# Mixing's x loaded behind the store that frees its place, and more passes ahead of two waits, in a four-layer graph kernel

## The chip, the cores and the metric

The kernel runs on one core of a Trainium2 chip. Its time is the device time of that core in microseconds: 1966.11 us (median of three runs, 1965.88 to 1972.42). The profile is one execution with a span of 1961.8 us.

## The reference, cut to what matters

x is [8 batches, 2048 nodes, 64 features] and adj is a [2048, 2048] matrix of zeros and ones. Four graph layers follow one another, each as x = layernorm(x + layer(x)). The change lies in layer 0, with layer 1 beside it:

```python
# layer 0, its end
deg = max(adj.sum(-1), 1)
industry = einsum('nm,bmf->bnf', adj / deg, x @ W_ind)
g = einsum('bne,benf->bnf', coefs1, elu(all_he))        # from the hyperedges
pair = stack([industry, g])
coefs2 = softmax(tanh(pair @ fcW + fcb) @ av)           # over the two
out = coefs2[0] * industry + coefs2[1] * g
x = layernorm(x + out)
# layer 1
A = adj + I;  dinv = rsqrt(A.sum(1))
x = layernorm(x + (dinv * A * dinv) @ x @ W.T)
```

Layer 2 is a Chebyshev graph convolution with an adaptive adjacency, layer 3 runs three message-passing steps.

## The kernel before, in words

The adjacency stays on chip as 16 row tiles. Batches go in pairs p (four pairs, two batches of 64 features on 128 partitions), nodes in four chunks c of 512. Each x value is split into two parts for the matmuls (v0h/v0l to v3h/v3l, one pair of tiles for each chunk), so a product of a pair with the adjacency is 2 groups g of 64 matmuls in layer 0 (tiles ug) and as many again in each pair of layer 1 (tiles u). Each such matmul is called a **pass** here: `products` (L323) and `layer1` (L988) are generators that give one pass at a time, and `fill(n)` (L401) runs the next n passes between other work. TensorE's order is therefore written out by hand.

Two helpers place the other engines' work. `after(n, f, ...)` runs f when n further passes have been given (L298), and `pin` keeps an instruction in program order on its engine. DMA issues on SP, and instructions that are not pinned, are placed by the framework's planner, by its own estimate of when they are ready; the finished list of each engine is then run in order. A tile name with `bufs=2` has two places; a third tile of that name waits until the first is no longer used.

Stages that matter here:

- **Hyperedges** (about 100 to 230 us). For each node tile, g is made by TensorE (pz), VectorE (L774 to L783), ScalarE and GpSimd, and scattered to `gs_hbm` by an indirect DMA (L786). Passes of the products run between. Inside the products, `inverses` (L340) turns the degrees: TensorE transposes them (pdc), VectorE adds one (L347), GpSimd makes the power -1/2 (dinv, L348), VectorE takes the maximum with one and the reciprocal (L349, L350), and after 8 passes TensorE transposes them again (pinv), from where they go to `inv_hbm`.
- **Mixing** (about 234 to 505 us), 16 steps i, each one pair and chunk. `mix_load` fetches products and inverse degrees; `mix_ind` makes industry on TensorE (pi) and VectorE (L866); `mix_g` loads g (gn) and x (r), transposes g (pg) and copies it (gt, L881); `mix_scores` makes four matmuls pf in two halves, with tanh on ScalarE (L895), GpSimd's ind - gt (L902) and VectorE's differences (L900); `mix_weigh` makes pd and the weight (L912, L914); `mix_end` transposes back (pt), adds to r (add_up, L933), and normalizes r (L834 to L846, with GpSimd's power ln_r at L843) and stores it as x1 (L925). r also needs r += gn on GpSimd (L883), which `mix_g` asks for 8 passes after itself.
- **Layer 1** starts at about 314 us between mixing's steps. `l1_parts` loads x1 (y, L945), scales it on GpSimd (L948) and splits it on ScalarE (L166) and VectorE (L167). After 64 passes ScalarE copies the sums (ut, L1011) and `l1_end` multiplies them by W (po) and adds x1 (L967, L968), with another layernorm.

The loop (L1029) runs scores(i), end(i-1), load(i+2), ind(i+1), g(i+1), weigh(i), with 8 or 9 passes behind each part. The end of a step takes 18 passes from mix_end to the store.

Of the kernel before, what the change touches and what calls it, by code (L numbers as in the profile page):

```python
# [30 lines left out]
F32 = mybir.dt.float32  # L31
# [6 lines left out]
ALU = mybir.AluOpType  # L38
# [18 lines left out]
def tile_gnn_fast(  # L57
# [23 lines left out]
    nc = tc.nc  # L81
# [3 lines left out]
    P = 128  # L85
# [3 lines left out]
    NCH = N // C  # L89
    JT = C // P  # L90
# [12 lines left out]
    def evacuate(dst, src):  # L103

        turn[0] ^= 1
        if turn[0]:
            nc.scalar.copy(dst, src)
        else:
            nc.vector.tensor_copy(dst, src)
# [60 lines left out]
    def mm(*args, **kw):  # L170
        tc.keep_in_program_order(nc.tensor.matmul(*args, **kw))  # L171
# [40 lines left out]
    def adj_c(t, c):  # L212

        return adj[t][c // 2][:, cols(c % 2)]
# [69 lines left out]
    def load_x(dst, p, c, eng=nc.sync):  # L284

        load = eng.dma_start(dst, x_n[p, c])
        if eng is nc.gpsimd:
            tc.keep_in_program_order(load)
# [9 lines left out]
    def after(n, f, *more):  # L298

        soon.append([n, lambda: (f(), after(*more) if more else None)])  # L300
# [22 lines left out]
    def products():  # L323

        deg1 = hy.tile([P, NT], F32, name="deg1")

        def degrees(g):
            du = pph.tile([P, 2, C], F32, tag="ph", name=f"du{g}", bufs=2)
            for t in range(NT):
                for i in range(2):  # L330
                    mm(
                        du[:, i, :], lhsT=ones_r, rhs=adj_c(t, 2 * g + i), start=t == 0, stop=t == NT - 1
                    )
                    yield
            for i in range(2):
                c = 2 * g + i
                r = slice(c * P // NCH, (c + 1) * P // NCH)
                evacuate(deg4[r, :], du[r, i, :])

        def inverses():  # L340

            pdc = places["small"]([P, JT, P], "pdc")
            for j in range(JT):
                transpose(pdc[:, j, :], deg4[:, cols(j, P)])
            pdc = pdc.rearrange("p j (c r) -> p c j r", c=NCH)[:, :, :, 0]
            d1 = deg1.rearrange("p (c j) -> p c j", c=NCH)
            nc.vector.tensor_scalar(d1, pdc, 1.0, None, op0=ALU.add)  # L347
            nc.gpsimd.tensor_tensor(dinv, deg1, neg_half[:, :NT], ALU.pow)  # L348
            nc.vector.tensor_scalar(d1, pdc, 1.0, None, op0=ALU.max)  # L349
            nc.vector.reciprocal(deg1, deg1)  # L350
            for _ in range(8):
                yield
            for c in range(NCH):
                pt = places["small"]([P, C], "pinv")
                for j in range(JT):
                    k = c * JT + j
                    transpose(pt[:, cols(j, P)], deg1[:, k:k + 1].to_broadcast([P, P]))
                row = va.tile([P, C], F32, tag="ut", name="inv", bufs=2)
                nc.scalar.copy(row, pt)
                nc.sync.dma_start(inv_hbm[:, cols(c)], row)  # L360
                for _ in range(4):
                    yield

        for p in range(NP):
            for g in range(2):
                own = (2 * g, 2 * g + 1)
                ug = pph.tile([P, 2, C], F32, tag="ph", name="ug", bufs=2)
                u = {c: ug[:, c % 2, :] for c in own}
                turning = inverses() if p == 0 and g == 1 else iter(())
                for t in range(NT):  # L370
                    for i in range(2):
                        for c in own:
                            mm(
                                u[c], lhsT=part[t // JT][i][:, t % JT, :], rhs=adj_c(t, c),
                                start=t == 0 and i == 0, stop=t == NT - 1 and i == 1,
                            )
                            tick()
                            if t > 1:
                                next(turning, None)
                            yield  # L380
                    if p == NP - 1 and g == 1 and t % JT == JT - 1:
                        first_parts(t // JT, free)
                    if p + 1 < NP and t % JT == JT - 1:
                        c = t // JT
                        if g == 1:
                            parts(p + 1, c)
                        if g == 1 and c < 2 or g == 0 and c >= 2:
                            fetch(p + 1, (c + 2) % NCH)
                if p == NP - 1:

                    for t in range(g * NT // 2, (g + 1) * NT // 2):
                        onto_diagonal(t, nc.gpsimd, ALU.add)
                for c in own:
                    ut = va.tile([P, C], F32, tag="ut", name="ut", bufs=2)
                    nc.scalar.copy(ut, u[c])
                    nc.sync.dma_start(u0_hbm[p][:, cols(c)], ut)
                if p == 0 and g == 0:
                    yield from degrees(0)
                    yield from degrees(1)

    def fill(n):  # L401
        for _ in range(n):
            if next(filler, None) == "wait":
                tick()
# [11 lines left out]
    with tc.tile_pool(name="pa_ps", bufs=1, space=PSUM) as pps:  # L416
# [75 lines left out]
        gts = so.tile([P, BINS], F32, name="gts")  # L492
# [32 lines left out]
        for t in range(NT // 2):  # L525
            for k in range(2):
                r = slice(k * E, (k + 1) * E)
# [271 lines left out]
    mp = mix_scope.enter_context(tc.tile_pool(name="mix", bufs=1, side="right"))  # L799
# [12 lines left out]
    def wide(c):  # L812
        return slice(c * JT, (c + 1) * JT)

    uts, invs, gts, inds, tts, rs = {}, {}, {}, {}, {}, {}
    xn, done, stored, due = [], [0] * NP, set(), set()


    pin = tc.keep_in_program_order
# [30 lines left out]
    steps = NP * NCH  # L850
# [17 lines left out]
    def mix_g(i):  # L868

        p, c = divmod(i, NCH)  # L870
        gn = mp.tile([P, JT, P], F32, tag="gn", name="gn", bufs=2)
        nc.sync.dma_start(
            gn, gs_hbm.rearrange("(p t) f -> p t f", t=NT)[:, wide(c), p * P:(p + 1) * P]
        )
        rs[i] = mp.tile([P, JT, P], F32, tag="r", name="r", bufs=2)
        load_x(rs[i], p, c)
        pg = lps.tile([P, C], F32, tag="mm", name="pg", bufs=4)
        for j in range(JT):
            transpose(pg[:, cols(j, P)], gn[:, j, :])
        gts[i] = mp.tile([P, C], F32, tag="gt", name="gt", bufs=2)  # L880
        pin(nc.scalar.activation(gts[i], pg, AF.Identity, bias=-1.0))  # L881
        r = rs[i]
        after(8, lambda: pin(nc.gpsimd.tensor_tensor(r, r, gn, ALU.add)))  # L883

    def mix_scores(i):

        t1 = []
        for src in (inds[i], gts[i]):
            for b in range(2):

                s = slice(b * F, (b + 1) * F)
                pf = lps.tile([P, C], F32, tag="mm", name="pf", bufs=4)
                mm(pf, lhsT=fc2[s, :], rhs=src[s, :], start=True, stop=True)
                t1.append(mp.tile([P, C], F32, tag="t1", name="t1", bufs=4))
                pin(nc.scalar.activation(t1[-1], pf, AF.Tanh, bias=fcb_col))  # L895
        tts[i] = t1[0:2]

        def differences():
            for b in range(2):
                pin(nc.vector.tensor_tensor(t1[b], t1[b], t1[2 + b], ALU.subtract))  # L900

        pin(nc.gpsimd.tensor_tensor(inds[i], inds[i], gts[i], ALU.subtract))  # L902
        after(5, differences)

    def mix_weigh(i):

# [10 lines left out]
    def mix_end(i):  # L917
        p, c = divmod(i, NCH)
        r = rs.pop(i)
        pt = lps.tile([P, C], F32, tag="mm", name="pt", bufs=4)  # L920
        for j in range(JT):
            transpose(pt[:, cols(j, P)], inds[i][:, cols(j, P)])

        def end():
            nc.sync.dma_start(x1_hbm[p][:, wide(c), :], r)  # L925
            stored.add((p, c))
            if p == 0:
                first_parts(c, mixed)
            elif (p, c) in due:
                l1_parts(p, c)  # L930

        def add_up():
            pin(nc.vector.scalar_tensor_tensor(  # L933
                r, pt.rearrange("p (t f) -> p t f", f=P), 0.5, r, op0=ALU.mult, op1=ALU.add
            ))

        after(3, add_up, 0, *normalized(mp, r, r, False, end))
# [85 lines left out]
    mix_load(1)  # L1023
    fill(24)
    mix_ind(0)
    fill(12)
    mix_g(0)
    fill(4)
    for i in range(steps + 1):  # L1029
        k = 9 if i > NCH else 8  # L1030
# [299 lines left out]
    for p in range(NP):  # L1330
        for c in range(NCH):
            r = staged("r").rearrange("p t (b f) -> p t b f", f=F)
# [923 lines left out]
```

## Time and profile before

| what | value |
|---|---|
| time, median of 3 | 1966.11 us |
| span of the profile | 1961.8 us |
| TensorE busy | 1867.9 us (95%) |
| VectorE / GpSimd / ScalarE busy | 1004.3 / 529.5 / 392.7 us |
| mean granted TensorE clock | 0.984 |
| r += gn (L883) | 16 times, 1284 ns (median) |
| load of x (L286 into r) and store of x1 (L925) | 16 times each, 256 KB |

A row of a timeline names start, duration, engine, line, operation, the tile written and the tiles read; in brackets stands how long the engine had been idle and what ended that. A row of waits gives total microseconds, times, and the longest. A window row gives, after its length, the busy time of TensorE, of its weight loads, of VectorE, ScalarE and GpSimd, then the granted TensorE clock, the DMA share and GB/s. Where TensorE is at 10.00 in a window of 10 us, nothing else matters there; the interest is in the windows where it isn't.

### The profile page before, as it was taken

The numbers are of one execution on the slowest core, as the hardware profiler recorded it, in microseconds if no ns is written. First come the engines' busy times: TensorE is split into PE (matmuls) and PEld (weight loads), VectorE is DVE, ScalarE is ACT, GpSimd is POOL, SyncE is SP. The second block draws the span as 40 slices with busy tenths as digits, with TensorE's granted clock in tenths as the row PEclk, the third lists the DMA queues.
The fourth block names the chain that finished last, engine by engine and source line by source line (L and its number), as shares of the span: only waits on it lengthen the run. The fifth ranks groups of instructions, "written<-read, shape, count | busy, mean of one in ns | idle before, by whom it ended". The sixth has DMA issues, their size and how long they took to land.

```text
span 1961.8 us, 19565 instructions
## 1 busy us (share of the span) xinstructions
PE 1867.9 (95%) x7100; PEld 1211.1 (62%) x7100; DVE 1004.3 (51%) x1741; ACT 392.7 (20%) x771; POOL 529.5 (27%) x480
## 2 busy tenths in 40 slices
PE   6888899888899999999999999999999999999997
PEld 4666565555754444855665575566547787877875
DVE  7789555565532211356556736754785343343332
ACT  1455343333222121100000000000002121222211
POOL 3678644454454434311001101100001020100201
PEclk9999899999999999999999999999999999999999
DMA  9923333432500000311101111111111122121211
GB/s 322 308 87 107 121 129 126 127 118 80 175 6 27 25 3 22 119 38 60 48 33 43 57 52 33 46 57 35 43 33 35 43 55 54 44 54 49 54 27 24
DMA packets 94185, 143.10 MB, mean 73 GB/s; under 512 B 29232, under 2 KB 40112, under 8 KB 93696
## 3 DMA queue, kind: packets, MB, share of 16 engines
q1 hardware_dynamic: 83920, 105.39, 17.7%
q0 software_dynamic: 7760, 27.66, 4.2%
q10 hardware_dynamic: 2400, 8.72, 1.2%
q8 instruction: 58, 0.95, 0.2%
q14 instruction: 47, 0.39, 0.1%
HBM read 98.67 MB, written 43.06 MB: 72 GB/s over the span
## 4 chain that ended last, share of the span: by engine, by line
PE 76%; DMA 4%; POOL 3%; DVE 3%; issue 2%; ACT 1%; SPq 0%; POOLq 0%; ACTq 0%; DVEq 0%
PE u L171 34%; PE py L171 22%; PE ua L171 11%; PE pr L171 2%; PE ug L171 2%; POOL ln_r L843 1%; DMA x_hbm<-r 1%; PE po L171 1%; DMA r<-in_x_n 1%; PE pf L171 1%; PE pt L174 1%; PE s L171 1%; DVE r L846 0%; DMA gs_hbm<-acc,order 0%; POOL r L968 0%
## 5 line engine op out<-in xcount | busy, mean ns | idle before, releaser
L171 PE MATMUL py<-wp,xg 128*128 128x512 f32 x1024 | 475.2, 592 | 0.7 <-DMA xg<-u_hbm 0.7
L171 PEld LDWEIGHTS py<-wp,xg 128*128 128x128 f32 x1024 | 193.3, 189 | 161.4 <-issue 138.8
L1343 DVE TENSOR_TENSOR fcav<-py,emb_n 128x512 f32<-128x512 f32 x256 | 176.9, 691 | 135.0 <-PE py L171 129.1
L171 PE MATMUL ua<-pt,xn 128*128 128x512 f32 x512 | 230.2, 592 | 1.5 <-DVE pt L1124 1.5
L1344 DVE TENSOR_REDUCE r<-fcav 128x32 f32<-128x512 f32 x256 | 175.5, 686 | 8.2
L171 PEld LDWEIGHTS ua<-pt,xn 128*128 128x128 f32 x512 | 96.9, 190 | 111.2 <-issue 104.2
L154 POOL TENSOR_TENSOR ln_r<-ln_e,neg_half 128x8 f32<-128x8 f32 x32 | 53.5, 1671 | 399.4 <-DVE ln_e L152 370.0
L171 PE MATMUL u<-adj,v0h 128*128 128x512 f32 x384 | 147.7, 452 | 1.3 <-ACT h L1499 1.3
L171 PE MATMUL u<-adj,v2l 128*128 128x512 f32 x384 | 141.0, 432 | 1.3 <-DVE v2l L167 1.3
L171 PE MATMUL u<-adj,v2h 128*128 128x512 f32 x384 | 141.3, 434 | 0.0
L171 PE MATMUL u<-adj,v1h 128*128 128x512 f32 x384 | 140.8, 434 | 0.0
L171 PE MATMUL u<-adj,v0l 128*128 128x512 f32 x384 | 139.8, 431 | 0.0
L171 PE MATMUL u<-adj,v3l 128*128 128x512 f32 x384 | 138.9, 426 | 0.0
L171 PE MATMUL u<-adj,v1l 128*128 128x512 f32 x384 | 138.4, 427 | 0.0
L171 PE MATMUL u<-adj,v3h 128*128 128x512 f32 x384 | 138.4, 427 | 0.0
L1124 DVE TENSOR_SCALAR pt<-pt 128x512 f32<-128x512 f32 x64 | 30.3, 473 | 150.5 <-ACT pt L1123 150.3
L1130 POOL TENSOR_TENSOR acc<-acc,pt 128x512 f32<-128x512 f32 x60 | 76.5, 1275 | 107.0 <-DVE pt L1124 106.4
L1425 DVE SCALAR_TENSOR_TENSOR ar<-fcav,ar 128x512 f32<-128x512 f32 x64 | 46.8, 731 | 108.7 <-ACT ar L1424 108.7
L171 PEld LDWEIGHTS u<-adj,v0h 128*128 128x128 f32 x384 | 71.0, 189 | 36.7 <-issue 24.1
L171 PEld LDWEIGHTS u<-adj,v2l 128*128 128x128 f32 x384 | 72.8, 191 | 31.9 <-issue 15.9
L171 PEld LDWEIGHTS u<-adj,v1l 128*128 128x128 f32 x384 | 72.9, 190 | 29.3 <-issue 14.4
L171 PEld LDWEIGHTS u<-adj,v3l 128*128 128x128 f32 x384 | 72.1, 188 | 29.4 <-issue 14.9
(360 smaller groups left out, 2717.2 us busy)
## 6 DMA issues: line engine op xcount, KB each, us to landing
adj<-in_adj_t POOLq DMA_DIRECT2D x32, 512.0 KB, 8.0
fcav<-in_adj_t SPq DMA_DIRECT2D x64, 256.0 KB, 2.9
u_hbm<-ut SPq DMA_DIRECT2D x48, 256.0 KB, 2.8
xg<-u_hbm SPq DMA_DIRECT2D x96, 128.0 KB, 2.9
x_hbm<-r SPq DMA_DIRECT2D x28, 256.0 KB, 2.2
hs_hbm<-st ACTq DMA_DIRECT2D x8, 584.0 KB, 5.4
xt<-in_x_t SPq DMA_DIRECT2D x16, 256.0 KB, 6.1
ut<-u_hbm SPq DMA_DIRECT2D x16, 256.0 KB, 3.4
```

Of the source, the lines that this page charges most:

```text
L154: nc.gpsimd.tensor_tensor(rstd, vare, neg_half[:, :groups], ALU.pow)
L171: tc.keep_in_program_order(nc.tensor.matmul(*args, **kw))
L174: tc.keep_in_program_order(nc.tensor.transpose(dst, src, ident))
L843: pin(nc.gpsimd.tensor_tensor(rstd, vare, neg_half[:, :groups], ALU.pow))
L1124: nc.vector.tensor_scalar(pt, pt, 1.0, None, op0=ALU.max)
L1130: nc.gpsimd.tensor_tensor(accs[c], accs[c], pt, ALU.add)
L1343: nc.vector.tensor_tensor(pr, py, e_b, ALU.mult)
L1344: nc.vector.tensor_reduce(r[:, j, b, cols(k, OH)], pr, AX.X, ALU.add)
L1425: nc.vector.scalar_tensor_tensor(ar.bitcast(F32), seen_a, 1.0, ar.bitcast(F32), op0=ALU.mult, op1=ALU.not_equal, accum_out=left[:, t, k:k ...
```

## The change

It has three parts. The load of x for step i+2 (new `mix_x`) is written directly behind the store of step i, whose place it takes, and not in `mix_g`; the add r += gn moves with it, from 8 passes after `mix_g` to 8 passes after `mix_scores`. This is for GpSimd not to stand before an x that is still on its way. The passes between the inverse degrees' arithmetic and their transposes become 20, for VectorE to finish first. And 28 passes instead of 12 run ahead of the first `mix_g`, while the last rows of g are still being written and read back.

```diff
@@ inverses
-            for _ in range(8):
+            for _ in range(20):
                 yield
@@ mix_g
-        rs[i] = mp.tile([P, JT, P], F32, tag="r", name="r", bufs=2)
-        load_x(rs[i], p, c)
+        gns[i] = gn
...
-        r = rs[i]
-        after(8, lambda: pin(nc.gpsimd.tensor_tensor(r, r, gn, ALU.add)))
+
+    def mix_x(i):
+        if i < steps:
+            rs[i] = mp.tile([P, JT, P], F32, tag="r", name="r", bufs=2)
+            load_x(rs[i], *divmod(i, NCH))
@@ mix_scores
         after(5, differences)
+        r, gn = rs[i], gns.pop(i)
+        after(8, lambda: pin(nc.gpsimd.tensor_tensor(r, r, gn, ALU.add)))
@@ mix_end, end
             nc.sync.dma_start(x1_hbm[p][:, wide(c), :], r)
+            mix_x(i + 2)
@@ ahead of the loop
     mix_ind(0)
-    fill(12)
+    fill(28)
     mix_g(0)
+    mix_x(0)
+    mix_x(1)
     fill(4)
```

More of the change, by code (lines that the diff above doesn't have):

```diff
@@ L813, in wide @@
         return slice(c * JT, (c + 1) * JT)
-    uts, invs, gts, inds, tts, rs = {}, {}, {}, {}, {}, {}
+    uts, invs, gts, gns, inds, tts, rs = {}, {}, {}, {}, {}, {}, {}
     xn, done, stored, due = [], [0] * NP, set(), set()
```

## The prediction

> **What bounds the kernel now.** I read the engine totals first, then the windows of 10 us, the waits between 240 and 510 us, and last the timelines around single stalls.
>
> ```profile
> PE 1867.9 (95%) x7100; PEld 1211.1 (62%) x7100; DVE 1004.3 (51%) x1741; ACT 392.7 (20%) x771; POOL 529.5 (27%) x480
> ```
>
> TensorE is busy for 1867.9 of 1961.8 us and its order is written out by hand, so the kernel gets faster only by what its idle time (93.9 us) and its slow-clock time lose. By windows, 24.6 us of the idle time lie before 100 us, 52.8 between 100 and 600, 16.5 later. The edits act between 120 and 505 us. In that stretch I compare windows:
>
> ```profile
> 230.00:240.00 10.00, 4.94 (x19) 3.45 (x17) 2.13 (x8) 1.67 (x3) 0.08 (x1) 0.76 0.53 178
> 260.00:270.00 10.00, 10.00 (x45) 6.12 (x44) 5.62 (x9) 4.60 (x8) 4.09 (x4) 1.00 0.37 120
> 370.00:380.00 10.00, 2.79 (x15) 2.17 (x13) 4.36 (x8) 3.21 (x6) 5.57 (x5) 0.76 0.25 79
> 420.00:430.00 10.00, 6.28 (x25) 4.34 (x22) 3.60 (x5) 2.94 (x5) 6.82 (x5) 0.83 0.30 91
> ```
>
> The second column is TensorE; no other engine is near 10 where TensorE has holes. So the mixing stage has no full engine: its holes are waits in a row. Which waits:
>
> ```profile
> POOL r L883 <- DMA r<-in_x_n: 71.3, 12, 7.0
> DVE r L846 <- POOL ln_r L843: 24.7, 15, 7.8
> ACT v1h L166 <- POOL y L948: 13.6, 3, 6.6
> PE po L171 <- ACT ut L1011: 11.0, 4, 7.2
> POOL r L968 <- DMA x<-x_hbm: 6.8, 2, 4.4
> ```
>
> GpSimd's add r += gn (L883) waits for x in 12 of 16 steps, 5.9 us each, with whatever is pinned behind it on GpSimd standing still. The largest hole, read from its start:
>
> ```profile
> 365.98 0.41 SPq L286 DMA_DIRECT2D r<-in_x_n  x1
> 370.17 1.29 POOL L883 TENSOR_TENSOR r<-r,gn 128x512 f32<-128x512 f32 x1 [6.01 <-DMA r<-in_x_n]
> 372.64 2.04 POOL L948 TENSOR_TENSOR y<-y,dinv 128x512 f32<-128x512 f32 x2
> 373.71 0.62 ACT L166 CAST v1h<-y 128x512 fp32r<-128x512 f32 x1 [6.58 <-POOL y L948]
> 378.32 1.07 ACT L1011 COPY ut<-u 128x512 f32<-128x512 f32 x2
> 378.95 2.08 PE L171 MATMUL po<-bd_w,ut 128*128 128x128 f32 x8 [7.21 <-ACT ut L1011]
> ```
>
> x lands at 370; GpSimd then scales y, ScalarE casts it, VectorE's pinned row moves on, ScalarE copies ut, and TensorE, which needed ut at 371.7, starts at 378.95.
>
> **What the Trainium skill says.** "Trainium Architecture — The Big Picture", Inside one NeuronCore: each engine has its own instruction stream and they meet only in semaphores. The chain above agrees: one waiting add held four engines. "DMA: Bandwidth & Descriptors", Anatomy of one DMA: about 2.0 us fixed, most of it the receipt of the last write; here the store of x1 (256 KB) lands in 2.1 us and the load of x in 2.65, when the queue is free. Same page, Two DMAs through the same engine are not ordered: a dependent DMA must wait for the first one's completion. So the load cannot overlap the store that frees its place: 2.1 + 2.65 = 4.75 us before and after. "TensorE: Matmul & The Clock Gate", Part 1: after an idle window of about 3.4 us the clock halves until some 3.4 us of work. The trace agrees roughly: the 8 matmuls of po at 378.95 took 2.08 us against 1.05 elsewhere; but holes of 1 to 2 us (471.6, 459.7) slowed it too.
>
> **The change part by part.**
>
> 1. Inverse degrees, 8 to 20 passes. A pass is one matmul of the products, 0.234 us (pairs start 0.467 apart).
>
> ```profile
> 126.81 0.17 DVE L349 TENSOR_SCALAR deg<-pdc 128x16 f32<-128x16 f32 x1 [4.72 <-POOL dinv L348]
> 127.89 0.62 PE L174 MATMUL pinv<-ident,deg 128*128 128x128 f32 x4 [2.89 <-DVE deg L350]
> ```
>
> Twelve passes are 2.8 us, so the 2.89 us wait in front of pinv goes. VectorE's own 4.72 us behind GpSimd's power stay, for L349 overwrites what the power reads and nobody moves it. TensorE then loses another 1.03 us at 130.1 and about 3.4 us to slow rows until 136 (pz 0.80 and 0.63 for 0.39). VectorE, full afterwards (9.6 to 10.0 of 10 from 140 to 190), idled 0.53 + 3.50 us for these late pz; that 4 us is what the stage can win. Low end 0: the filler is interleaved with pz, whose places VectorE frees, so TensorE could meet the same 126.8. High end 4. I take 3.
>
> 2. Sixteen passes more ahead of mix_g(0).
>
> ```profile
> 237.41 1.08 PE L174 MATMUL pg<-ident,gn 128*128 128x128 f32 x4 [5.06 <-DMA gn<-gs_hbm]
> ```
>
> These are 3.7 us moved, not added: every pass is run once, so the hole shrinks from 5.06 to 1.3 us. The rows after it were slow until 243 (1.08 for 0.60, 1.20 for 0.72, 2.05 for 1.13: 2.3 us); with a short hole I keep half. Gain 3.7 + 1.1 = 4.8. It has one danger: 16 passes also reach the release of v0, so the next load of xc, which must wait for GpSimd's v0l, is now written ahead of gn and may stand before it on SP. Then gn starts near 238 and the gain is gone. I take 4.3, from 0 to 6.
>
> 3. x loaded behind the store; the add moved to 8 passes after mix_scores. Written order today, in passes from mix_end(i-1) with 9 passes a part: mix_g(i+1) at 9, the add at 17, the store that frees its x at 18. The add thus stands ahead of the very store whose place its load needs, and the DMA pair (4.75 us) is always open: 5.9 us a time. Afterwards the add stands at 9 + 9 + 9 + 8 = 35, that is 17 passes (4.0 us) and the eight pf matmuls (1.9 us, 301.39 to 303.31) behind the store: 5.9 us for 4.75. It is late only when SP is. No operation is added: 16 adds (1.28 us), 16 loads stay. r is needed by add_up one whole step later (some 36 passes, 8 us), so the later add costs nothing there. The place of gn is held longer, but its next load is not needed for over 30 passes; on SP such a load waited for this add (51.8 us in all), which held up x1 and y loads behind it, for instance 449.77. The load of x still holds SP for the store's 2.1 us, as now.
> What it is worth: after 310 us TensorE waits 26.3 us in the mixing (7.21 at 379, 3.72 at 427, 3.09 at 404, 2.22 at 327, 1.95 at 450, 1.90 at 501, 1.30 at 460, 1.11 at 443, seven below 1). Followed back, the five largest each reach an add of L883. Slow rows after them, each against its normal length (pd 2.48 for 1.08, pt 1.11 for 0.60, pf 2.19 for 1.02 and the like), add up to 8.9 us. Of 35.2 us I take 70%, 24.6, since the pinned rows still have waits of their own (ln_r on ln_e 34.2 us, L968 on x1 6.8), which can come last once this one is gone. From 40% (14) to 100%.
> The 4.09 us before pb at 510.85 stay: they wait for an embedding load into the space that mixing frees at its end.
>
> Sum: 3 + 4.3 + 24.6 = 31.9; 1966.1 - 31.9 = about **1934**.
>
> **Rivals.**
> - The next wait takes the place (1951): 40% of the third part (14) and little of the two others (1), 15 us. For it: GpSimd also waits for x1, and the scaled y stands in the same row. Against: GpSimd is busy only 4 to 5 of 10 there, and SP's late x1 loads stood behind the add too.
> - All of it (1918): 4 + 6 + 35.2 + 3 from the tail, 48 us. For it: from 240 to 310 us, with no layer-1 work mixed in, TensorE has no hole at all. Against: twelve layer-1 ends with tight distances of 4 to 9 passes remain.
> - The loads get a worse place (slower, 1977): if x stands on SP behind y and x1 loads that wait (one row held it 9.5 us at 449.77), the add or, a step on, VectorE's add_up waits; four more holes of 4 us, minus part 1 and 2's 5, are +11. Mixing is also 16 passes (3.7 us) later against layer 1's last pass: v3l ended at 518.66, 2.8 us before its first matmul at 521.47. Against: the store of x is followed at once by its load already, and the written order now matches that.
>
> **How the numbers follow.** Forecast 0.57, next wait 0.22, all of it 0.10, worse place 0.06, nothing measurable 0.05. The range 1919 to 1957 takes in nearly all of "all of it" and the next-wait case, and leaves the slow one out. Half a per cent is 9.8 us (1956.3 to 1975.9): faster takes the first three less a tail of 0.02, 0.87; same 0.08; slower 0.05.
>
> **What would show it.** The 71.3 us of L883 on x should fall under 15, pg's wait to about 1.3, pinv's to near 0, the 7.21 us at po go, and the windows from 310 to 500 us show 10.00 for TensorE in most rows at clock 1.00. Wrong if VectorE or ScalarE waits for GpSimd's L968 instead, if SP's wait ahead of the x load grows beyond 26 us, or if gn(0) is issued after an xc load.

## The result, and the profile after

| | before | after |
|---|---|---|
| time, median (lowest to highest), 4 runs each | 1965.99 us (1961.19 to 1972.42) | 1934.43 us (1932.57 to 1936.43) |
| ratio | | 0.9838 (95%: 0.9807 to 0.9868) |
| span of the profile | 1961.8 us | 1931.4 us |
| mean granted TensorE clock | 0.984 | 0.986 |

The forecast was 1934 us, the range 1919 to 1957. The engine totals after:

```profile
PE 1863.2 (96%) x7100; PEld 1211.2 (63%) x7100; DVE 1010.8 (52%) x1741; ACT 393.9 (20%) x771; POOL 533.5 (28%) x480
```

The instruction counts are those of before, so nothing was added or saved: the same 7100 matmuls have less air between them. TensorE's idle time went from 93.9 to 68.2 us (1931.4 - 1863.2), 25.7 less; its busy time, for the same matmuls, fell by 4.7. Together these are the 30.4 us of the span. By stages, the stretch from the last scatter of g to layer 2's first matmuls (tile s) went from 315.3 to 283.4 us (31.9 less). The hyperedges ahead of it gave about 1, and what lies ahead of them took 2.3 us longer in this execution.

The windows of 10 us that were shown of before, now of after; the second column is TensorE:

```profile
230.00:240.00 10.00, 10.00 (x44) 7.59 (x43) 2.13 (x8) 1.78 (x4) 2.03 (x2) 1.00 0.36 110
260.00:270.00 10.00, 10.00 (x44) 6.17 (x43) 5.87 (x10) 5.10 (x9) 6.38 (x6) 1.00 0.54 183
370.00:380.00 10.00, 9.55 (x37) 5.35 (x37) 5.96 (x9) 5.05 (x9) 8.97 (x7) 1.00 0.58 184
420.00:430.00 10.00, 10.00 (x47) 6.44 (x43) 7.53 (x11) 5.17 (x9) 7.44 (x7) 1.00 0.34 111
480.00:490.00 10.00, 8.06 (x23) 6.62 (x24) 6.17 (x10) 2.10 (x5) 3.03 (x2) 0.50 0.90 298
```

The one at 260 had been full before. Of the three with holes two are full now and the one at 370 is at 9.55, all at clock 1.00. The fifth lies behind a hole at pb, the matmuls of the embeddings for layer 2: the clock stood at 0.50 there. Before, pb had a hole of 4.09 us at its own place; it is 4.90 now. Two longer windows, first of before and then of after, hold most of the gain:

```profile
310.00:450.00 140.00, 120.08 (x522) 78.02 (x521) 79.14 (x116) 46.74 (x82) 66.86 (x54) 0.95 0.38 120
```

```profile
310.00:450.00 140.00, 139.36 (x635) 91.83 (x634) 102.68 (x142) 56.62 (x98) 85.71 (x63) 1.00 0.44 140
450.00:500.00 50.00, 41.49 (x180) 32.37 (x179) 29.68 (x49) 13.14 (x25) 20.14 (x15) 0.86 0.48 163
```

In the same 140 us TensorE now runs 635 matmuls and not 522, with 0.64 us idle for 19.92. From 450 to 500 it is idle for 8.5 us, in two holes: 3.61 us at pt and 4.90 at pb. Some of the waits between 240 and 510 us after:

```profile
POOL ln_r L843 <- DVE ln_e L842: 33.6, 15, 5.5
POOL r L907 <- DMA r<-in_x_n: 27.8, 9, 5.5
DVE r L846 <- POOL ln_r L843: 19.7, 18, 3.1
ACT v0h L166 <- POOL y L953: 9.9, 4, 3.3
PE pb L171 <- DMA xn<-in_emb: 4.9, 1, 4.9
PE pt L174 <- DVE ind L918: 3.6, 1, 3.6
```

The add (now L907) still waits for x, 27.8 us in 9 steps where it was 71.3 in 12. What changed is what stands behind it. Around the place of the old 7.21 us hole, in the timeline of after:

```profile
370.13 1.05 POOL L953 TENSOR_TENSOR y<-y,dinv 128x512 f32<-128x512 f32 x1
...
374.60 3.71 POOL L843 TENSOR_TENSOR ln_r<-ln_e,neg_half 128x8 f32<-128x8 f32 x2
375.55 0.38 SPq L929 DMA_DIRECT2D x_hbm<-r  x1
379.29 0.33 SPq L286 DMA_DIRECT2D r<-in_x_n  x1
382.21 1.28 POOL L907 TENSOR_TENSOR r<-r,gn 128x512 f32<-128x512 f32 x1 [2.65 <-DMA r<-in_x_n]
```

The store of x1 (L929) goes out at 375.55 and the load that takes its place at 379.29, 3.7 us later and not 2.1, because this store took 3.7 us to land. The add follows 6.66 us behind the store and waits 2.65. But the scaled y of layer 1 and the pinned powers ran ahead of it, so ScalarE and TensorE had their data in time.

### The profile page after: what moved, and what is told of

Read it like the earlier page. It is cut to its first block, busy times and chain, and to the rows that moved or that the text cites. A ratio compares the mean times of both kernels' runs of the same rounds, so it can differ in the third digit from the quotient of the medians.

```text
span 1931.4 us, 19557 instructions
## 1 busy us (share of the span) xinstructions
PE 1863.2 (96%) x7100; PEld 1211.2 (63%) x7100; DVE 1010.8 (52%) x1741; ACT 393.9 (20%) x771; POOL 533.5 (28%) x480
## 4 chain that ended last, share of the span: by engine, by line
PE 83%; DMA 2%; DVE 1%; issue 1%; POOL 1%; ACT 1%; POOLq 0%; SPq 0%; ACTq 0%; DVEq 0%
PE u L171 37%; PE py L171 23%; PE ua L171 11%; PE ug L171 3%; PE pr L171 2%; PE pf L171 1%; PE po L171 1%; PE pt L174 1%; PE s L171 1%; PE pd L171 1%; PE pi L171 1%; DMA x<-x_hbm 0%; PE pn L174 0%; DMA xn<-in_emb 0%; PE pg L174 0%
## 5 line engine op out<-in xcount | busy, mean ns | idle before, releaser
L171 PEld LDWEIGHTS u<-adj,v3h 128*128 128x128 f32 x384 | 72.8, 190 | 28.9 <-issue 14.3
```

## The experiments

A gain in microseconds is the difference of the two medians; the interval behind a ratio says how far it can be trusted. "8" and "20" are the passes ahead of the inverse degrees' transposes, "12" and "28" those ahead of the first `mix_g`. Experiments with the same time for the kernel before shared its runs.

**Third part alone.** The changed kernel with 8 and 12 passes.

```diff
-            for _ in range(20):
+            for _ in range(8):
-    fill(28)
+    fill(12)
```

> The kernel before with only the third part: x loaded behind the store, the add r += gn 8 passes after mix_scores; 8 and 12 passes as before. Theory (the add standing ahead of its load made TensorE's holes): some 24 us less than before, 1942 us, and TensorE's waits between 310 and 450 us under 2 us in all. Rival (the added passes carry the gain): less than 10 us under before.

Measured: 1940.34 us for 1966.27, ratio 0.9853 (0.9831 to 0.9876), 25.9 us less. The rival is out, but TensorE is still idle for 4.0 us between 310 and 450, not under 2:

```profile
310.00:450.00 140.00, 135.96 (x606) 88.03 (x604) 99.47 (x139) 54.13 (x95) 81.39 (x62) 0.99 0.43 136
```

**Both counts alone.** The kernel before with 20 and 28 passes.

```diff
-            for _ in range(8):
+            for _ in range(20):
-    fill(12)
+    fill(28)
```

> The kernel before with only the two added stretches of passes (20 and 28). Theory: 3 us from the inverse degrees, of which the profile after suggests only about 1, and 4 to 5 us from the first gathered rows: 1959 to 1962 us, with the holes after 310 us as before (26 us). Rival: most of the gain is here, under 1945 us.

Measured: 1962.97 us, ratio 0.9987 (0.9978 to 0.9996), 3.3 us less. The first pg waits 1.2 us for 5.06, as priced, but pt's longest wait grew from 3.7 to 5.5 us, and GpSimd's wait for x stayed:

```profile
POOL r L883 <- DMA r<-in_x_n: 63.9, 11, 6.5
```

**Only the add moved.** In the kernel before, the add goes to 8 passes after `mix_scores`; the load stays written in `mix_g`.

```diff
@@ mix_g
-        r = rs[i]
-        after(8, lambda: pin(nc.gpsimd.tensor_tensor(r, r, gn, ALU.add)))
+        gns[i] = gn
@@ mix_scores
+        r, gn = rs[i], gns.pop(i)
+        after(8, lambda: pin(nc.gpsimd.tensor_tensor(r, r, gn, ALU.add)))
```

> The kernel before with only the add moved to 8 passes after mix_scores; the load of x stays written in mix_g, passes as before. Theory: the planner had put the load right behind the store already, so the written place of the load is worth nothing, and this equals the third part alone, about 1942 us. Rival (the load's place is what helps): close to before, 1960 us or more.

Measured: 1936.82 us, ratio 0.9843 (0.9822 to 0.9865), 29.5 us less. Its window has nearly the matmuls of after:

```profile
310.00:450.00 140.00, 136.13 (x613) 88.76 (x611) 101.93 (x140) 53.97 (x94) 82.94 (x63) 1.00 0.43 138
```

**Only the load moved.** The changed kernel with 20 and 28 passes and the load behind its store, but the add pinned one pass behind its load (the first two steps as in the change).

```diff
@@ mix_scores
-        after(8, lambda: pin(nc.gpsimd.tensor_tensor(r, r, gn, ALU.add)))
+        if i < 2:
+            after(8, lambda: add_g(i))
@@ mix_end, end, behind mix_x(i + 2)
+            if i + 2 < steps:
+                after(1, lambda: add_g(i + 2))
```

> The kernel after, but the add stands one pass behind the load of its x, and not 17 passes (from step 2 on). Theory: GpSimd again waits for most loads, some 4 us a time and over 50 us in all, and about the gain of the third part is lost: 1950 to 1960 us. Rival (load behind store is enough, wherever the add stands): equal to after, 1934 us.

Measured: 1962.10 us, ratio 0.9977 (0.9968 to 0.9986), a little more than the 1950 to 1960 expected. What is left is what the two counts gave alone (0.9987, 0.9978 to 0.9996). The third part's gain is gone, the wait is back (L888 is the add), and so are the holes:

```profile
POOL r L888 <- DMA r<-in_x_n: 75.0, 13, 6.6
```

```profile
310.00:450.00 140.00, 121.05 (x513) 78.53 (x512) 77.04 (x115) 46.86 (x82) 66.24 (x53) 0.95 0.38 120
```

These two together say that the add's place is all of the third part, within the spread. Where the load is written is worth nothing that can be measured: before, SP already issued it as soon as the store had landed, or at most 0.6 us later.

**A third place for r.** The kernel before with add and load where they were, and one buffer more: the load then needs no store of the step just ending.

```diff
-        rs[i] = mp.tile([P, JT, P], F32, tag="r", name="r", bufs=2)
+        rs[i] = mp.tile([P, JT, P], F32, tag="r", name="r", bufs=3)
```

> The kernel before, add and load where they were, 8 and 12 passes, but r with three places instead of two, so that the load of x for a step no longer waits for the store of the step before last, but for one a whole step older. Theory (the wait for x is what costs, whatever takes it away): GpSimd's 71 us on x fall under 15 and the gain is that of the moved add, 1935 to 1942 us. Rival (the add costs by its place in GpSimd's row, not by waiting, or SP brings the loads late all the same): 1955 us or more.

Measured: 1939.01 us for 1967.99, ratio 0.9858 (0.9834 to 0.9881), 29.0 us less. No wait of the add on x is left in GpSimd's list, which now begins so:

```profile
POOL ln_r L843 <- DVE ln_e L842: 54.6, 16, 6.5
POOL ind L902 <- PE pf L171: 22.1, 6, 11.8
```

The add was not moved here, and the gain is the same. It was therefore the open DMA pair in GpSimd's row, and not something else about the add's old place.

**The add later still.** The changed kernel with 15 passes for 8.

```diff
-        after(8, lambda: pin(nc.gpsimd.tensor_tensor(r, r, gn, ALU.add)))
+        after(15, lambda: pin(nc.gpsimd.tensor_tensor(r, r, gn, ALU.add)))
```

> The kernel after, with the add 15 and not 8 passes behind mix_scores. Theory: the 27.8 us that GpSimd still waits for x are reached with nothing urgent behind them; they fall under 10 us and the time stays, 1932 to 1936 us. Rival: they still cost TensorE something, and the time falls under 1930 us.

Measured: 1932.89 us for 1965.72, ratio 0.9836 (0.9815 to 0.9857). The wait on x fell from 27.8 to 15.0 us, not under 10; the time is that of after. So what is left of that wait costs nothing that can be measured.

**One count at a time on top of the third part.** The changed kernel with 20 and 12, and with 8 and 28.

```diff
@@ 20 and 12
-    fill(28)
+    fill(12)
@@ 8 and 28
-            for _ in range(20):
+            for _ in range(8):
```

> The kernel after with 12 passes ahead of the first mix_g again: the third part and the 20 passes of the inverse degrees. Theory (the inverse degrees' passes only trade TensorE's wait for a wait at pz, since VectorE still stands 4.7 us behind GpSimd's power): within 2 us of the third part alone, 1937 to 1941 us. Rival (my forecast's 3 us): 1935 to 1937 us.

> The kernel after with 8 passes at the inverse degrees: the third part and the 28 passes ahead of the first mix_g. Theory: the 5 us hole ahead of the first pg goes, but layer 1 is then 16 passes further when mixing ends, and holes near the end of mixing (450 to 490 us) give most of it back: 1935 to 1940 us, with over 7 us of hole and slow rows there. Rival (no link between both ends of mixing): 1932 to 1935 us and those holes under 4 us.

Measured beside 1968.35: 1932.79 us (1932.30 to 1939.08), ratio 0.9835 (0.9814 to 0.9856), for 20 and 12; 1938.43 us (1934.87 to 1940.43), 0.9851 (0.9828 to 0.9874), for 8 and 28. 8 and 28 came out as expected; 20 and 12 came out below both guesses, which stays unexplained. The intervals overlap, with each other and with that of 8 and 12. TensorE's waits between 230 and 510 us show why 28 passes bring so little. With 20 and 12:

```profile
PE pg L174 <- DMA gn<-gs_hbm: 5.4, 1, 5.4
PE po L171 <- ACT ut L1016: 2.8, 3, 2.0
PE pf L171 <- DVE ind L866: 1.8, 1, 1.8
PE pb L171 <- DMA xn<-in_emb: 1.0, 1, 1.0
```

After has 0.8 us at pg and none at po and this pf, but 4.9 at pb and 3.6 at pt. The hole at the front of the mixing went, and two at its end came. From the last scatter of g to layer 2's first matmuls the two kernels take 282.8 and 283.4 us.

**The inverse degrees in a tile of their own.** The changed kernel; the maximum and the reciprocal no longer overwrite what GpSimd's power reads.

```diff
-            nc.vector.tensor_scalar(d1, pdc, 1.0, None, op0=ALU.max)
-            nc.vector.reciprocal(deg1, deg1)
+            nc.vector.tensor_scalar(d2, pdc, 1.0, None, op0=ALU.max)
+            nc.vector.reciprocal(deg2, deg2)
```

> The kernel after, with the maximum and the reciprocal of the degrees in a tile of their own, so that VectorE need not wait until GpSimd's power has read the degrees. Theory: VectorE's 4.7 us there go, the hyperedge stage ends 2 to 4 us earlier, 1931 to 1933 us. Rival: another engine of that stage sets its pace (GpSimd is at 8 to 9 of 10), and nothing changes: 1934 us.

Measured beside 1968.35: 1933.59 us, ratio 0.9828 (0.9809 to 0.9847). The time can't be told from that of after. VectorE's 4.73 us wait is gone, but the hyperedges, 2 to 4 us shorter by the theory, take 122.8 us for 123.8, and TensorE's row shows another hole:

```profile
141.51 1.11 PE L174 MATMUL pinv<-ident,deg 128*128 128x128 f32 x4 [3.05 <-DVE y L780]
```

**More passes ahead of the embeddings.** The changed kernel, with 56 for 32 passes ahead of pb.

```diff
-    fill(32)
+    fill(56)
```

> The kernel after, with 56 passes and not 32 between the end of mixing and the first of layer 2's embedding chunks. Theory (the hole of 4.9 us before pb and its 4 us of slow rows are an embedding load that is 20 passes late): both go, 1926 to 1929 us. Rival: the hole only moves to where the embeddings are used first, 1933 us or more.

Measured beside 1968.35: 1935.82 us, ratio 0.9844 (0.9825 to 0.9862). A miss. pb no longer waits; po does:

```profile
491.50 0.33 ACTq L991 DMA_DIRECT2D xn<-x_hbm  x1
491.87 0.37 ACT L1097 COPY bias<-pb 128x256 f32<-128x256 f32 x1 [8.16 <-DMA x_hbm<-r]
492.14 0.59 ACT L1016 COPY ut<-u 128x512 f32<-128x512 f32 x1
492.78 2.08 PE L171 MATMUL po<-bd_w,ut 128*128 128x128 f32 x8 [6.88 <-ACT ut L1016]
```

Here ScalarE itself issues a load (L991) of x2, layer 1's result, and that load waits for the last x2 store to land. Its copies of bias and ut stood behind the issue, with ScalarE idle for 8.16 us, and TensorE behind ut. The hole only moved.

**Shorter parts in mixing's first steps.** The 16 passes that 28 takes from the parts later on are taken from steps 0 to 3 instead (7 passes a part for 8), so that layer 1 is where it was when the mixing ends; once alone, once with the separate inverse degrees.

```diff
-        k = 9 if i > NCH else 8
+        k = 9 if i > NCH else 8 if i == NCH else 7
```

> The kernel after, with 7 passes and not 8 behind each part of mixing's steps 0 to 3: the 16 passes added ahead of mix_g(0) are taken back (15 of them) before layer 1 begins, so that layer 1 stands to mixing's end as in the kernels with 12 passes. Theory (the hole before pg is won and given back at the end of mixing, where layer 1's last pair is 16 passes further): the waits of 3.6 us at pt and of about 5 us at pb go, pg keeps no hole, 1925 to 1930 us. Rival (those holes come from something else): they stay, 1933 us or more.

> As aligned, with the maximum and the reciprocal of the degrees in a tile of their own. Theory: 1 us less than aligned, since that stage of degrees_apart was 0.7 us shorter than that of after; rival: no different from aligned, or more, when the pinv transposes then meet another wait (3 us in degrees_apart).

Measured beside 1965.72: 1931.53 us, ratio 0.9823 (0.9801 to 0.9844), and 1932.56 us, 0.9832 (0.9811 to 0.9854). In both pt's wait fell from 3.6 to 0.74 us; pb's fell from 4.9 to 2.3 in the one and 1.0 in the other. But po waited 3.2 us in both and pf 2.0 and 2.2 in their place. The 1925 to 1930 hoped for did not come, and no version can be told from after.

## Why the prediction was right, step by step

**The third part (24.6 us).** The mechanism held: the add stood ahead of the store whose place its load needs, with GpSimd's row behind it. Three ways to take that wait away, in kernels with 8 and 12 passes, give 25.9, 29.5 and 29.0 us (their intervals reach from 23 to 35 us together); putting the add back beside its load takes the gain away. By the medians 74 to 84% of the 35.2 us came, for the 70% that were priced; by the intervals the term may also have been right. The next waits in the row (ln_r on ln_e, 34.2 us before and 33.6 after) took nothing over, because TensorE has 0.64 us idle where they lie.

Four details were wrong. First, not each of the five largest holes led back to an add. The one of 3.09 us at pf is there unchanged with three places for r, where no add waits for x; in both TensorE waits for VectorE's ind. First of before, then with three places:

```profile
403.71 1.13 PE L171 MATMUL pf<-ind,fcav 64*128 64x512 f32 x4 [3.09 <-DVE ind L866]
```

```profile
392.91 1.75 PE L171 MATMUL pf<-ind,fcav 64*128 64x512 f32 x4 [3.09 <-DVE ind L866]
```

Second, the 4.09 us before pb were to stay. Before, and with three places:

```profile
PE pb L171 <- DMA xn<-in_emb: 4.1, 1, 4.1
```

```profile
PE pb L171 <- DMA xn<-in_emb: 0.9, 1, 0.9
```

With the third part in the kernel of 8 and 12 passes they are 2.7, with only the add moved nothing is left. So the third part wins there too, 1.4 to 4.1 us that its price left out.

Third, the wait on x was to fall under 15 us and is 27.8. The prediction set 17 passes and eight matmuls of written order, 5.9 us, against a store and a load of 4.75. But GpSimd does not wait for passes: it comes to the add when the instruction ahead of it in its row is done. In the nine steps that wait, that was between 0.6 us before the store's issue and 4.2 us behind it, and the add could run 4.9 to 7.8 us behind the store. The longest of them:

```profile
317.16 1.29 POOL L904 TENSOR_TENSOR ind<-ind,gt 128x512 f32<-128x512 f32 x1
319.02 0.32 SPq L929 DMA_DIRECT2D x_hbm<-r  x1
321.14 0.33 SPq L286 DMA_DIRECT2D r<-in_x_n  x1
323.91 1.30 POOL L907 TENSOR_TENSOR r<-r,gn 128x512 f32<-128x512 f32 x1 [5.47 <-DMA r<-in_x_n]
```

In the kernels with 12 passes ahead of the first `mix_g` and the add moved the same wait is 12.8 to 16.6 us; why it is longer with 28 is open. The prediction treated it as the measure of the gain. It is not, as the later add shows: the length of a wait counts only with what is queued behind it.

Fourth, SP's wait ahead of the gn load, which the prediction counted with the harm that the add does, did not shrink. First of before, then of after:

```profile
SPq L872 <- POOL r L883: 51.8, 14, 5.7
```

```profile
SPq L872 <- POOL r L907: 53.4, 14, 8.3
```

**The inverse degrees (3 us).** They brought some 2 us. From the first scatter of g to the last, the hyperedges take 122.9 to 124.4 us in the seven kernels with 20 passes and degrees in one tile (mean 123.4), and 124.7 to 126.6 in the five with 8 (mean 125.4). pinv's 2.89 us did go, but the wait came out again at the next rows, for VectorE's 4.73 us stayed, as the prediction said:

```profile
129.16 0.17 DVE L349 TENSOR_SCALAR deg<-pdc 128x16 f32<-128x16 f32 x1 [4.73 <-POOL dinv L348]
129.43 0.27 PE L174 MATMUL pslot<-ident,hrow 128*64 128x128 f32 x1 [1.62 <-issue]
130.69 0.50 PE L171 MATMUL pz<-hrh,ident_r 128*128 128x512 f32 x1 [0.99 <-DVE y L778]
```

**The 16 passes (4.3 us).** The hole at the first pg went whole, where 1.3 us were to be left, without the feared xc load ahead of gn on SP:

```profile
239.12 0.63 PE L174 MATMUL pg<-ident,gn 128*128 128x128 f32 x4
```

But the net worth is small. Alone, both counts gave 3.3 us (0.8 to 4.3) for 7.3; on top of the third part, 28 for 12 made no difference that the runs separate, in either pair of kernels. The step that failed is "moved, not added": the term took the 3.7 us as won at the front and put the cost of their absence later on at nothing. With the third part, pb waits 0 to 2.7 us in the four kernels with 12 passes and 4.9 to 5.2 in the four with 28 and nothing else done about it, and the longest wait at pt is up to 0.7 us in the one set and 2.5 to 3.6 in the other. A pass run ahead of the first `mix_g` is missing later, so layer 1's last pair is 16 passes further when the mixing ends, and its scaled y and casts stand in the rows of GpSimd and ScalarE ahead of the last steps' work:

```profile
457.03 1.50 POOL L953 TENSOR_TENSOR y<-y,dinv 128x512 f32<-128x512 f32 x1
458.56 0.62 ACT L166 CAST v0h<-y 128x512 fp32r<-128x512 f32 x1 [1.97 <-POOL y L953]
459.09 0.59 ACT L916 ACTIVATE th<-pd 128x512 f32<-128x512 f32 x1
460.62 0.68 DVE L918 SCALAR_TENSOR_TENSOR ind<-th,ind 128x512 f32<-128x512 f32 x1
461.36 0.66 PE L174 MATMUL pt<-ident,ind 128*128 128x128 f32 x4 [3.61 <-DVE ind L918]
```

y is late, its cast holds ScalarE until 459.1, th comes behind it, and TensorE's pt at 461.36. At pb the embedding load is late, and the row runs slow until 489.5: 7.57 us for pb and 13 passes that take 1.03 + 3.04 elsewhere, 3.5 us more. The two kernels with shorter first parts wait 0.74 us at pt. That the passes' shift is behind pt's wait is thus shown; how much of pb's delay comes from it is open, since shorter parts left 2.3 us of it in one kernel and 1.0 in the other.

That the forecast of 1934 hit within 1 us is luck. By the medians two errors cancel: the third part was about 1 to 5 us too small, the two others some 2 to 5 us too large (7.3 us priced; 3.3 alone, and 2.1 to 5.7 as what is left of 31.6 us beside the third part's 29.5 and 25.9). The second error is clear of the noise with both counts alone; the first is not, in two of its three measurements. The rival "next wait takes the place" is ruled out for the third part and is what happened to the second. The rival "the loads get a worse place" did not come: the kernel is faster.

## What to carry to other kernels

On an engine that runs its row in order, an instruction ahead of the transfer that it depends on costs what stands behind it, and not its own 1.28 us: put it behind work that the engine really has to wait for until store and load are done, or give the tile one more place, which did the same here with one digit. When a hole at the front of an overlap is filled with work taken from further on, look at the far end, where that work will be missing. And test a wait's worth by what starves behind it: the same add waited 27.8 us after at no price that could be measured, and 71.3 us before at a price of 26 to 30. Passes counted in the written order are a clock for TensorE alone; another engine comes as early as its own row lets it.

## What the runs showed of the hardware

- A DMA issued from ScalarE's queue held ScalarE's own instructions until the store that it waited for had landed: with 56 passes ahead of pb, a copy stood 8.16 us behind it.
- A store of 256 KB took 2.1 us to land in some steps of after (319.02) and up to 5.0 us in others (327.72).
- What slows TensorE's clock was not the length of one hole alone. In the kernel before, a hole of 1.30 us at 459.69 was followed by pairs of passes at 1.05 us for 0.63 until 463.7; in the kernel with only the add moved, one of 2.10 us at 392.51 was not (0.63 from 394.99 on), nor one of 3.09 us at 403.71 in the kernel before (0.63 from 406.67 on). The Trainium skill ("TensorE: Matmul & The Clock Gate", Part 1) speaks of an idle window of about 3.4 us; the hole of 1.30 us is shorter and was followed by slow rows all the same, and these runs do not show what else counts.

```profile
459.69 1.34 PE L171 MATMUL pf<-gt,fcav 64*128 64x512 f32 x2 [1.30 <-ACT th L912]
461.98 1.05 PE L171 MATMUL u<-adj,v2h 128*128 128x512 f32 x2
```

- A third buffer for a tile of 256 KB and a later place of one instruction were worth the same within the spread (29.0 and 29.5 us).
